# Splitting a carried projection over two positions, and loading the first band ahead of most weights, in a windowed-attention and convolution kernel

## The chip, the cores and the metric

The kernel runs on one core of one Trainium2 chip, as one launch. The metric is the device time in microseconds. The kernel before took 3295.52 us in the median of three runs (3294.91 to 3316.36).

## The reference

Input x is 4 x 128 x 128 x 128 (image, channel, row, column), float32. Layer 0 cuts each image into 9 x 9 overlapping regions of 16 x 16 pixels (step 14) and runs attention in each; overlaps are averaged. A projection, a depthwise convolution with batch statistics and a second projection follow. Layer 1 is two quantised 3 x 3 convolutions.

```python
y = _ln(tok, ln1_g, ln1_b)
qkv = y @ w_qkv                       # q, k, v; 4 heads of 32 channels
attn = softmax(einsum('bhqd,bhkd->bhqk', q, k) * hd ** -0.5)
o = einsum('bhqk,bhkd->bhqd', attn, v)
tok = o @ w_out + b_out + tok
xf = merge(tok)                       # overlaps averaged
y = _ln(xf, ln2_g, ln2_b) @ w_p0 + b_p0          # 128 -> 256 channels
ym = depthwise_conv5x5(y, dw_k)
ym = gelu(gelu(batchnorm(ym)))
x1 = ym @ w_p2 + b_p2 + xf
out = bn(conv3x3(q4(bn(conv3x3(q4(x1), q4(w1)))), q4(w2))) + x1
```

## The kernel before

Channels lie on the 128 partitions. An image is worked in nine bands of 16 rows (t = 0 to 35 over the four images), a band in nine regions from left to right, called positions 0 to 8 here. Within the loop over t and j the order of work is written by hand: PE, ACT, DVE and SP run their instructions in program order (MANUAL, L39), POOL is scheduled. Per position: scores (L684), exponential on ACT (L692), sums of pairs on POOL and DVE (L702), the values of the position before (L747, L755, L767 to L774), and, for every second position, v for two regions (L670).

Beside the attention of band t, the function beside(t) hangs other work on the positions, as four lists each: after the scores, after the sums, and two at the end. That other work is

- ln1_chunks(t+1), two chunks a1 and a2 of nine steps: squares, variance, deviation, spread, second, then q and k projections (L458). The layernorm's per-pixel scale goes to DRAM from ACT's queue (row, L374) and comes back spread over all partitions through SP (xn, L379); L388 multiplies it in.
- post_chunks(t-1), two chunks b1 and b2 of eleven steps: the output projection (L510, L511), the second layernorm, then four p0 steps, each one projection with wp0 (L526), a copy from PSUM on ACT into one of four y buffers (L531), and a store of it to y2_d. y_00 and y_10 are the first row half, y_01 and y_11 the second. A y buffer is used again four p0 steps later and must have been stored by then.
- the depthwise convolution of an image whose bands are done, conv_steps: a first step that loads two tiles (begin), then steps that load two ahead and multiply (L611), copy (L618), take statistics (L622) and store (cv_d). Images 0 and 1 are spread over nine bands each (t from 10 and from 19), image 2 over five bands (t from 28); the last image's first part starts at t=33, its second at t=35. A band in which such a list is begun is called fresh.

The four p0 steps of b2 do not fit into their own band: beside() returns them in the list left, and the next call takes them as f. For t above 9, f stands whole in position 0, and the p0 steps of b1 stand in position 8. For t up to 9 another list (full) places them.

All of these share three PSUM banks called pm (ps_m). SP issues almost all DMAs in program order, a step's stores after the step that follows it (run, flush).

Ahead of the loop, L120 to L160 load weights and vectors, fold scales, biases and the layernorm's centring into wqkv and wp0 on PE and DVE with tiles and PSUM of their own; then the first x blocks are loaded (L412) and ln1_chunks(0) runs, its two chunks step by step in turn.

Of the kernel before, what the change touches and what calls it, by code (L numbers as in the profile page):

```python
# [8 lines left out]
F32 = mybir.dt.float32  # L9
F8 = mybir.dt.float8e4  # L10
AF = mybir.ActivationFunctionType
ALU = mybir.AluOpType
# [34 lines left out]
def layers(  # L47
# [52 lines left out]
    def vector(v, name):  # L100
        n = v.shape[0] // P
        t = const.tile([P, n], F32, name=name)
        nc.sync.dma_start(out=t, in_=v.rearrange("(h p) -> p h", p=P))
        return t
# [15 lines left out]
    nc.sync.dma_start(out=wqkv, in_=w_qkv)  # L120
    g1, b1 = vector(ln1_g, "g1"), vector(ln1_b, "b1")
    wo = const.tile([P, P], F32, name="wo")
    nc.sync.dma_start(out=wo, in_=w_out)
    bo = vector(b_out, "bo")
    g2, b2 = vector(ln2_g, "g2"), vector(ln2_b, "b2")
    wp0 = const.tile([P, 2, P], F32, name="wp0")
    nc.sync.dma_start(out=wp0, in_=w_p0.rearrange("p (h m) -> p h m", h=2))
    bp0 = vector(b_p0, "bp0")

    with (
        tc.tile_pool(name=f"prep_{tag}", bufs=1) as prep,
        tc.tile_pool(name=f"ps_p_{tag}", bufs=1, space=PSUM) as ps_p,
    ):
        center = prep.tile([P, P], F32, name="center")
        nc.vector.tensor_scalar(center, ident, -1.0 / P, None, ALU.add)
        nc.vector.tensor_scalar(wqkv[:, :P], wqkv[:, :P], float(HD) ** -0.5, None, ALU.mult)
        pb = ps_p.tile([P, 8], F32, name="pb")  # L140
        qb = const.tile([P, 1], F32, name="qb")
        nc.tensor.matmul(pb[:, 0:1], wqkv[:, :P], b1, start=True, stop=True)
        nc.vector.tensor_copy(qb, pb[:, 0:1])
        bv = prep.tile([P, 1], F32, name="bv")
        nc.tensor.matmul(pb[:, 1:2], wqkv[:, 2 * P :], b1, start=True, stop=True)
        nc.vector.tensor_copy(bv, pb[:, 1:2])
        nc.tensor.matmul(pb[:, 2:3], wo, bv, start=True, stop=True)
        nc.vector.tensor_tensor(bo, pb[:, 2:3], bo, ALU.add)
        for h in range(2):
            nc.tensor.matmul(pb[:, 3 + h : 4 + h], wp0[:, h, :], b2, start=True, stop=True)  # L150
        nc.vector.tensor_tensor(bp0, pb[:, 3:5], bp0, ALU.add)
        nc.vector.tensor_scalar(wqkv, wqkv, g1, None, ALU.mult)
        nc.vector.tensor_scalar(wp0, wp0, g2, None, ALU.mult)

        for w in (wqkv, wp0.rearrange("p h m -> p (h m)")):
            n = w.shape[1]
            pw = ps_p.tile([P, 3 * P], F32, name="pw")
            nc.tensor.matmul(pw[:, :n], center, w, start=True, stop=True)
            nc.vector.tensor_copy(w, pw[:, :n])


    quad = const.tile([P, HEADS], F32, name="quad")
# [12 lines left out]
    with ExitStack() as actx:  # L175
# [22 lines left out]
        def scratch(n):  # L198

            return up.tile([P, 32 * CW], F32, name="u")[:, :n]  # L200
# [208 lines left out]
        def load_rows(pool, name, t, r, n):  # L409
            b, i = bands[t]  # L410
            xt = pool.tile([P, LB * P], F32, name=name)
            nc.sync.dma_start(  # L412
                out=xt[:, : n * P].rearrange("p (r c) -> p r c", c=P),
                in_=x[b, :, i * STEP + r : i * STEP + r + n, :],
            )
            return xt
# [364 lines left out]
        def beside(t):  # L781

            one = list(early) if t else ln1_chunks(1)
            early[:] = ln1_chunks(t + 2) if t + 2 < T else []
            two = post_chunks(t - 1) if t else []
            had = len(todo)
            if t >= 2:
                b, i = bands[t - 2]  # L790
                if i == NR - 1 and b < B - 1:
                    todo.extend(conv_steps(b))
                    share[0] = NR if b < B - 2 else 5
                elif b == B - 1 and i == 4:
                    todo.extend(conv_steps(B - 1))
                    share[0] = 2
                elif b == B - 1 and i == 6:
                    todo.extend(conv_steps(B))
                    share[0] = 1

            fresh = len(todo) > had
            n = len(todo) // share[0] if fresh else -(-len(todo) // max(share[0], 1))
            conv = [todo.pop(0) for _ in range(n)]
            share[0] -= 1
            a1, a2 = one if one else ([None] * 9,) * 2
            b1, b2 = two if two else ([None] * 11,) * 2
            if t == T:
                return [
                    *conv, *left, *b1[:2], *b2[:2], b1[2], b1[3], b2[2], b2[3], b1[4], b2[4], b1[5], b2[5],
                    b1[6], *b1[7:], b2[6], *b2[7:],  # L810
                ]


            c = [[] for _ in range(NR)]
            d = [[] for _ in range(NR)]
            twice = len(conv) > NR
            for j in sorted((1, 3, 5, 7, 8, 4, 6, 2, 0)[: len(conv)]):
                c[j] = [conv.pop(0)]
                d[j] = [conv.pop(0)] if twice and j and conv else []
            x1 = lambda: fetch(t, 0)  # L820
            x2 = lambda: fetch(t, 1)
            f, left[:] = list(left), b2[7:]
            s1 = early[0][0] if early else None
            plan = [
                ([a1[1]], [], f, [*c[0], a1[2]]),
                ([], [a1[3], *c[1]], [], [a2[0]]),
                ([a2[1]], [a1[4]], b1[:2], [*c[2], a2[2]]),
                ([], [a2[3], *c[3]], [], [b1[2]]),
                ([b1[3]], [a2[4]], [*a1[5:], *b2[:2]], [*c[4], b1[4]]),
                ([], [b1[5], *c[5]], [], [b2[2]]),  # L830
                ([b2[3]], [b1[6]], a2[5:], [*c[6], b2[4]]),
                ([], [b2[5], x1, *c[7]], [], []),
                ([], [b2[6], x2], b1[7:], [*c[8], s1]),
            ]
            if t == 0:
                plan[0] = ([], [], [], [*c[0], *a1[:3]])
            if t <= NR:

                left[:] = [*b1[9:], *b2[7:]]
                full = (f[:3], f[3:], b1[:2], a1[5:7], a1[7:], b2[:2], a2[5:7], a2[7:], b1[7:9])  # L840
                plan = [(one, two, w, four) for (one, two, three, four), w in zip(plan, full)]
            return [(one, two, three, four + d[j]) for j, (one, two, three, four) in enumerate(plan)]
# [15 lines left out]
        share[0] = NR + 1  # L858
        for blk in row_blocks(0):
            xb[0, blk[0]] = load_rows(xp, "xt", 0, *blk)  # L860
        bng, bnb = vector(bn_g, "bng"), vector(bn_b, "bnb")
        wp2 = const.tile([P, 2, P], F32, name="wp2")
        nc.sync.dma_start(out=wp2, in_=w_p2.rearrange("(h p) m -> p h m", p=P))
# [2 lines left out]
        ga2, be2 = vector(gamma2, "ga2"), vector(beta2, "be2")  # L866
        with nullcontext() if safe else tc.manual_schedule(engines=MANUAL):
            ln1_begin(0)
            for steps in zip(*ln1_chunks(0)):
                run(steps)  # L870
            last = None
            for t in range(T):
                flush(len(stores))
                scores, halves, values_in, values = attention(t)
                if t + 1 < T:
                    ln1_begin(t + 1)
                for j, side in enumerate(beside(t)):
                    scores(j)
                    if last:
                        last()  # L880
                    run(side[0])
                    halves(j)
                    if j == 0 and t:
                        post_begin(t - 1)
                    run(side[1])
                    if j % 2 == 0:
                        values_in(j)
                    run(side[2])
                    run(side[3])
                    last = lambda j=j, values=values: values(j)  # L890
            last()
            post_begin(T - 1)
            flush(len(stores))

            bctx.close()
            tail += [actx.enter_context(tc.tile_pool(name=f"late{n}_{tag}", bufs=n)) for n in (1, 4)]
            all_w = [tail[0].tile([P, 3, 16, 32], F32, name=f"w{k}") for k in range(NCK)]
            for k in range(NCK // 2):
                weights(all_w[k], k, 0, 2, nc.sync.dma_start)
            run(beside(T))  # L900
            flush(len(stores))
            run(todo)
            for n, s in enumerate(conv_steps(len(units) - 1, 4, (all_w, tail[1]))):
                s()
                flush(len(stores), nc.scalar)
                if n < NCK // 2:
                    weights(all_w[NCK // 2 + n], NCK // 2 + n, 0, 2, nc.sync.dma_start)
            flush(len(stores))
# [381 lines left out]
```

## Time and profile before

| | us |
|---|---|
| median of three runs | 3295.52 |
| profiled execution | 3291.11 |
| its span | 3289.0 |
| first scores (L684) start | 33.13 |
| last band's first scores start | 2104.7 |
| PE idle before L526, all | 37.2 |
| PE idle before L684, all | 20.3 |
| ACT idle before L531, all | 146.1 |
| POOL busy | 828.3 |

The rows of the page below are read as line, engine, operation, output and inputs, shapes and count, then busy time and mean duration, then the idle time of that engine just before these instructions and what ended most of it. Idle time of an engine counts only where it holds up the one that sets the end.

```profile
L526 PE MATMUL pm<-xn,wp 128*128 128x512 f32 (+1 forms) x576 | 249.7, 565 | 37.2 <-ACT y L531 20.0
L531 ACT ACTIVATE y<-pm,bp 128x512 f32<-128x512 f32 (+1 forms) x288 | 183.0, 641 | 146.1 <-DMA y_d<-y 80.3
```

### The profile page before, as it was taken

To read this page: it belongs to the slowest core of one execution; us is meant where nothing else is said; L and a number is where in the kernel's file an instruction comes from. 1 tells how busy PE (TensorE), PEld (TensorE's weight loads), DVE (VectorE), ACT (ScalarE), POOL (GpSimd) and SP (SyncE) were. 2 spreads that over 40 slices of the span, in tenths; PEclk is the share of its full clock that TensorE was granted. 3 is DMA by queue.
4 is the path that set the end of the run, shared out by engine and by line. 5 is a ranking of instruction groups with operands and counts; after the bars stand their busy time and mean duration, and the time that the engine had idled before them with its cause. 6 is when DMAs were issued, how large, how long until landed. Compare 5 with 4: busy or idle time off the path is not lost.

```text
span 3289.0 us, 75777 instructions
## 1 busy us (share of the span) xinstructions
PE 3093.5 (94%) x30922; PEld 1541.3 (47%) x30922; DVE 2020.6 (61%) x3247; ACT 1992.0 (61%) x2670; POOL 828.3 (25%) x1042
## 2 busy tenths in 40 slices
PE   7999999999999999999998998884799999999998
PEld 4555554444544444544444444553444444444343
DVE  5777887776766667676555664542455555666543
ACT  5777776777777676777565564532477767333443
POOL 3444443333333333333222222210111111000000
PEclk9999999999999999999999998876699999999999
DMA  3455677888886788886899888766799999452298
GB/s 93 135 172 159 174 181 179 194 211 196 210 198 166 182 205 208 198 211 166 190 202 206 206 192 202 191 169 176 242 356 360 359 357 300 150 167 71 99 359 311
DMA packets 812363, 682.76 MB, mean 208 GB/s; under 512 B 581646, under 2 KB 696679, under 8 KB 812007
## 3 DMA queue, kind: packets, MB, share of 16 engines
q1 hardware_dynamic: 793447, 673.10, 74.8%
q10 hardware_dynamic: 18560, 4.72, 0.6%
q8 instruction: 247, 4.05, 0.5%
q14 instruction: 109, 0.89, 0.1%
HBM read 410.81 MB, written 270.81 MB: 207 GB/s over the span
## 4 chain that ended last, share of the span: by engine, by line
PE 77%; DMA 10%; ACT 5%; DVE 3%; SPq 2%; issue 2%; ACTq 0%; POOL 0%; DVEq 0%; POOLq 0%
PE pc L1064 19%; PE pm L611 9%; PE sc L684 9%; PE po L747 8%; PE pm L458 6%; PE pb L1122 6%; PE pm L526 5%; PE pm L670 4%; PE po L755 4%; DMA y_d<-y 3%; PE pm L510 3%; PE pm L357 3%; DMA xn<-row 2%; DMA cv_d<-c 2%; DMA u<-y_d 2%
## 5 line engine op out<-in xcount | busy, mean ns | idle before, releaser
L767 DVE RECIPROCAL rd<-po 128x256 f32<-128x256 f32 x324 | 569.3, 1757 | 451.2 <-PE po L755 448.3
L1064 PE MATMUL pc<-q,wq 128*128 128x512 fp8e4 x3168 | 702.0, 381 | 14.4 <-DVE q L1076 14.4
L692 ACT ACTIVATE pt<-sc 128x1024 f32<-128x1024 f32 x648 | 628.1, 1025 | 129.3 <-PE sc L684 65.1
L702 POOL TENSOR_TENSOR sm<-pt 128x512 f32<-128x512 f32 x324 | 412.9, 1274 | 1048.1 <-ACT pt L692 706.8
L1064 PEld LDWEIGHTS <-wq 128*128 128x128 fp8e4 x3168 | 309.0, 98 | 417.7 <-issue 50.2
L684 PE MATMUL sc<-q,kr 32*128 32x256 f32 x5184 | 405.1, 415 | 20.3 <-ACT pt L692 20.1
L611 PE MATMUL pm<-u,w 40*32 40x504 f32 (+5 forms) x7680 | 369.1, 504 | 33.8 <-DMA u<-y_d 20.8
L684 PEld LDWEIGHTS sc<-q,kr 32*128 32x128 f32 x5184 | 250.1, 190 | 259.3 <-issue 166.1
L747 PE MATMUL po<-pt,v 128*32 128x256 f32 x5184 | 361.5, 398 | 8.7 <-DVE part L771 7.7
L618 ACT COPY c<-pm 128x512 f32<-128x512 f32 (+1 forms) x256 | 132.0, 563 | 264.4 <-PE pm L611 254.4
L622 DVE BATCH_NORM_STATS2 st<-c 128x6 f32<-128x512 f32 (+2 forms) x384 | 174.6, 505 | 190.1 <-ACT c L618 189.5
L526 PE MATMUL pm<-xn,wp 128*128 128x512 f32 (+1 forms) x576 | 249.7, 565 | 37.2 <-ACT y L531 20.0
L531 ACT ACTIVATE y<-pm,bp 128x512 f32<-128x512 f32 (+1 forms) x288 | 183.0, 641 | 146.1 <-DMA y_d<-y 80.3
L458 PE MATMUL pm<-xn,wqkv 128*128 128x512 f32 (+1 forms) x576 | 251.5, 565 | 11.6 <-DVE xn L388 9.0
L702 DVE TENSOR_TENSOR sm<-pt 128x512 f32<-128x512 f32 x324 | 243.5, 751 | 29.7 <-ACT pt L692 29.5
L611 PEld LDWEIGHTS pm<-u,w 40*32 40x32 f32 x7680 | 145.2, 112 | 216.8 <-issue 161.4
L1122 PE MATMUL pb<-cv,wp 128*128 128x512 f32 x512 | 232.6, 598 | 11.4 <-ACT cv L1113 11.4
L747 PEld LDWEIGHTS po<-pt,v 128*32 128x32 f32 x5184 | 139.6, 111 | 182.7 <-issue 108.7
L1072 DVE BATCH_NORM_STATS2 st<-pc 128x6 f32<-128x512 f32 x256 | 165.6, 689 | 67.3 <-PE pc L1064 67.3
L755 PE MATMUL po<-sm,ones 128*32 128x256 f32 x2592 | 206.0, 390 | 0.0
L670 PE MATMUL pm<-wqkv,yr 128*128 128x128 f32 x1296 | 193.4, 290 | 0.0
L670 PEld LDWEIGHTS pm<-wqkv,yr 128*128 128x128 f32 x1296 | 159.0, 192 | 68.7 <-issue 44.4
(147 smaller groups left out, 3410.8 us busy)
## 6 DMA issues: line engine op xcount, KB each, us to landing
cv<-cv_d SPq DMA_DIRECT2D x64, 1024.0 KB
u<-y_d SPq DMA_DIRECT2D x224, 256.0 KB
cv_d<-c SPq DMA_DIRECT2D x192, 256.0 KB
xn<-row SPq DMA_DIRECT2D x80, 512.0 KB
y_d<-y SPq DMA_DIRECT2D x160, 256.0 KB
xfl<-xf_d SPq DMA_DIRECT2D x64, 512.0 KB
id_d<-y SPq DMA_DIRECT2D x64, 512.0 KB
idt<-id_d SPq DMA_DIRECT2D x64, 512.0 KB
```

The lines of the kernel that those rows point to most:

```text
L458: nc.tensor.matmul(pm[:, : n * P], wqkv[:, m * P : (m + 1) * P], held["xn"][hh], start=True, stop=True,)
L526: nc.tensor.matmul(pm[:, : n * P], wp0[:, h, :], held["xn"][hh], start=True, stop=True)
L611: nc.tensor.matmul(pc[half][32 * q : 32 * q + 32, j, :, a:z], wt[hs, s, c0 + c, :], ut[hs, :, c, a + s - 1 : z + s - 1], start=(s == 1), s ...
L670: nc.tensor.matmul(pv[:, m, c, :], region(yr, j + m)[:, c * P : (c + 1) * P], wqkv[:, 2 * P :], start=True, stop=True,)
L684: nc.tensor.matmul(sc[h // 2][:, h % 2, kc, :].rearrange("p (r c) -> p r c", c=RS), region(kr, j)[hs, kc * P : (kc + 1) * P], queries(j, h ...
L692: nc.scalar.activation(pt, sc[p], AF.Exp)
L702: add(sm, pt[:, :, 0, :], pt[:, :, 1, :], ALU.add)
L747: nc.tensor.matmul(po[hs, 0, :], v[:, kc, hs], pt[h // 2][:, h % 2, kc, :], start=(kc == 0), stop=(kc == 1),)
L755: nc.tensor.matmul(po[hs, 1, :], ones, sm[h // 2][:, h % 2, :], start=True, stop=True)
L767: nc.vector.reciprocal(rd, po[:, 1, :])
L1064: nc.tensor.matmul(pc[:, h], w[:, t, :], q1[b][:, r + dy : r + dy + RB, dx : dx + P], start=(t == 0), stop=(t == 8),)
L1122: nc.tensor.matmul(pb[:, m], wp2[:, h, :], cv[:, h, px], start=(h == 0), stop=(h == 1))
```

## The change

Three things are moved; no operation on data is dropped. The loads of wo, bo, g2, b2, wp0 and bp0 come after the first two x loads on SP. The folding of the weights becomes two functions: prepare_qkv runs after the first layernorm step of band 0, prepare_rest after the fourth; their PSUM is taken from pm and the centring matrix from a u buffer. And in beside(), for t above 9, the carried list f is cut into two steps for position 0 and the rest for position 2, ahead of the output projection there, except in a fresh band of the last image. In fresh bands the convolution's steps take positions 3, 5, 7, 8, 4, 6, 1, 2, 0 in this order of preference, instead of 1, 3, 5, 7, 8, 4, 6, 2, 0.

```diff
-    nc.sync.dma_start(out=wo, in_=w_out)
-    bo = vector(b_out, "bo")
-    g2, b2 = vector(ln2_g, "g2"), vector(ln2_b, "b2")
...
-    bp0 = vector(b_p0, "bp0")
...
+    def prepare_qkv(pb, pw, center):
+        nc.vector.tensor_scalar(wqkv[:, :P], wqkv[:, :P], float(HD) ** -0.5, None, ALU.mult)
         nc.vector.tensor_scalar(center, ident, -1.0 / P, None, ALU.add)
...
+        nc.tensor.matmul(pb[:, 1:2], wqkv[:, 2 * P :], b1, start=True, stop=True)
         nc.vector.tensor_copy(qb, pb[:, 0:1])
...
+        nc.vector.tensor_scalar(wqkv, wqkv, g1, None, ALU.mult)
+
+        nc.tensor.matmul(pw[:, : 3 * P], center, wqkv, start=True, stop=True)
+        nc.vector.tensor_copy(wqkv, pw[:, : 3 * P])
+
+    def prepare_rest(pb, pw, center):
+        w = wp0.rearrange("p h m -> p (h m)")
         nc.tensor.matmul(pb[:, 2:3], wo, bv, start=True, stop=True)
...
+        nc.tensor.matmul(pw[:, : 2 * P], center, w, start=True, stop=True)
+        nc.vector.tensor_copy(w, pw[:, : 2 * P])
...
-            for j in sorted((1, 3, 5, 7, 8, 4, 6, 2, 0)[: len(conv)]):
+            where = (3, 5, 7, 8, 4, 6, 1, 2, 0) if fresh else (1, 3, 5, 7, 8, 4, 6, 2, 0)
+            for j in sorted(where[: len(conv)]):
...
+            f0, f1 = (f, []) if fresh and bands[t - 2][0] == B - 1 else (f[:2], f[2:])
...
-                ([a1[1]], [], f, [*c[0], a1[2]]),
+                ([a1[1]], [], f0, [*c[0], a1[2]]),
                 ([], [a1[3], *c[1]], [], [a2[0]]),
-                ([a2[1]], [a1[4]], b1[:2], [*c[2], a2[2]]),
+                ([a2[1]], [a1[4]], [*f1, *b1[:2]], [*c[2], a2[2]]),
...
             xb[0, blk[0]] = load_rows(xp, "xt", 0, *blk)
+        nc.sync.dma_start(out=wo, in_=w_out)
+        bo = vector(b_out, "bo")
+        g2, b2 = vector(ln2_g, "g2"), vector(ln2_b, "b2")
+        nc.sync.dma_start(out=wp0, in_=w_p0.rearrange("p (h m) -> p h m", h=2))
+        bp0 = vector(b_p0, "bp0")
...
             ln1_begin(0)
-            for steps in zip(*ln1_chunks(0)):
+            center = scratch(P)
+            room = lambda: ps_m.tile([P, 512], F32, name="pm")
+            for n, steps in enumerate(zip(*ln1_chunks(0))):
                 run(steps)
+                if n == 0:
+                    prepare_qkv(room(), room(), center)
+                elif n == 3:
+                    prepare_rest(room(), room(), center)
```

More of the change, by code (lines that the diff above doesn't have):

```diff
@@ L122, in layers @@
     wo = const.tile([P, P], F32, name="wo")
-    nc.sync.dma_start(out=wo, in_=w_out)
-    bo = vector(b_out, "bo")
-    g2, b2 = vector(ln2_g, "g2"), vector(ln2_b, "b2")
     wp0 = const.tile([P, 2, P], F32, name="wp0")
-    nc.sync.dma_start(out=wp0, in_=w_p0.rearrange("p (h m) -> p h m", h=2))
-    bp0 = vector(b_p0, "bp0")
[L133 to L137, printed above, removed]
+    qb = const.tile([P, 1], F32, name="qb")
@@ L138, in layers @@
+    bv = const.tile([P, 1], F32, name="bv")
+    def prepare_qkv(pb, pw, center):
+        nc.vector.tensor_scalar(wqkv[:, :P], wqkv[:, :P], float(HD) ** -0.5, None, ALU.mult)
         nc.vector.tensor_scalar(center, ident, -1.0 / P, None, ALU.add)
-        nc.vector.tensor_scalar(wqkv[:, :P], wqkv[:, :P], float(HD) ** -0.5, None, ALU.mult)
-        pb = ps_p.tile([P, 8], F32, name="pb")
-        qb = const.tile([P, 1], F32, name="qb")
         nc.tensor.matmul(pb[:, 0:1], wqkv[:, :P], b1, start=True, stop=True)
+        nc.tensor.matmul(pb[:, 1:2], wqkv[:, 2 * P :], b1, start=True, stop=True)
@@ L143, in layers @@
         nc.vector.tensor_copy(qb, pb[:, 0:1])
-        bv = prep.tile([P, 1], F32, name="bv")
-        nc.tensor.matmul(pb[:, 1:2], wqkv[:, 2 * P :], b1, start=True, stop=True)
         nc.vector.tensor_copy(bv, pb[:, 1:2])
+        nc.vector.tensor_scalar(wqkv, wqkv, g1, None, ALU.mult)
[3 more added lines that the diff above has]
+        w = wp0.rearrange("p h m -> p (h m)")
@@ L147, in layers @@
         nc.tensor.matmul(pb[:, 2:3], wo, bv, start=True, stop=True)
-        nc.vector.tensor_tensor(bo, pb[:, 2:3], bo, ALU.add)
         for h in range(2):
             nc.tensor.matmul(pb[:, 3 + h : 4 + h], wp0[:, h, :], b2, start=True, stop=True)
+        nc.vector.tensor_tensor(bo, pb[:, 2:3], bo, ALU.add)
         nc.vector.tensor_tensor(bp0, pb[:, 3:5], bp0, ALU.add)
-        nc.vector.tensor_scalar(wqkv, wqkv, g1, None, ALU.mult)
         nc.vector.tensor_scalar(wp0, wp0, g2, None, ALU.mult)
[L155 to L159, printed above, removed]
+        nc.tensor.matmul(pw[:, : 2 * P], center, w, start=True, stop=True)
```

## The prediction

> **What bounds the kernel now.** I read the page's busy times first, then the list of waits, then a table by stretch of time, then the timeline of the worst stretch, and last the chain of waits there and at the start.
>
> ```profile
> PE 3093.5 (94%) x30922; PEld 1541.3 (47%) x30922; DVE 2020.6 (61%) x3247; ACT 1992.0 (61%) x2670; POOL 828.3 (25%) x1042
> ```
>
> TensorE is busy for 94% of a span of 3289.0 us, so about 195 us are idle, and only idle or half-speed PE time can be won by moving work that stays the same. The waits (engine and line, what released it: us in total, times, longest) tell which idle time the diff can touch:
>
> ```profile
> ACT y L531 <- DMA y_d<-y: 80.3, 64, 6.6
> PE sc L684 <- ACT pt L692: 20.1, 28, 3.7
> PE pm L526 <- ACT y L531: 20.0, 12, 4.5
> ```
>
> L526 is the carried projection, L531 its copy out of PSUM. That copy waits for an older store of the same y buffer to land, then PE waits for the copy. By stretch (us, busy time per engine with counts, granted clock, DMA share, GB/s), one undisturbed band (t=22) and bands 29 to 32:
>
> ```profile
> 1216.00:1273.00 57.00, 56.95 (x693) 28.69 (x692) 40.37 (x63) 41.24 (x63) 21.06 (x27) 1.00 0.85 205
> ...
> 1627.00:1704.00 77.00, 71.35 (x844) 34.27 (x836) 44.75 (x69) 44.83 (x69) 21.03 (x27) 0.93 0.92 202
> 1704.00:1778.00 74.00, 69.73 (x852) 33.13 (x836) 43.75 (x68) 44.63 (x69) 21.03 (x27) 0.95 0.91 204
> 1778.00:1859.00 81.00, 72.28 (x848) 34.16 (x844) 45.60 (x71) 44.87 (x70) 21.03 (x27) 0.94 0.91 203
> 1859.00:1930.00 71.00, 66.20 (x787) 32.23 (x788) 43.35 (x67) 43.62 (x67) 21.03 (x27) 0.95 0.89 207
> ```
>
> Band 22 is PE from end to end: nothing can be won there. Bands 29 to 32 have idle PE and a clock below full. Band 31's timeline shows how (start, us, engine, line; in brackets the idle time before):
>
> ```profile
> 1788.98 0.58 ACT L531 ACTIVATE y<-pm,bp 128x384 f32<-128x384 f32 x1 [5.61 <-DMA y_d<-y]
> ...
> 1789.62 1.39 PE L526 MATMUL pm<-xn,wp 128*128 128x384 f32 x2 [4.53 <-ACT y L531]
> ...
> 1797.93 0.58 ACT L531 ACTIVATE y<-pm,bp 128x384 f32<-128x384 f32 x1 [6.56 <-DMA y_d<-y]
> ...
> 1801.07 2.99 PE L684 MATMUL sc<-q,kr 32*128 32x256 f32 x16 [3.74 <-ACT pt L692]
> ```
>
> The first of the four copies waits 5.61 us, the last 6.56 us, and the Exp of position 1, queued behind it on ACT, is late by as much. The scores that follow take 2.99 us where an undisturbed group takes 1.15: half clock. The chain of waits names the same stores:
>
> ```profile
> 1785.79 4.89 DMA y_d<-y
> ...
> 1791.27 6.58 DMA y_d<-y
> ```
>
> **What the Trainium skill says.** "TensorE: Matmul & The Clock Gate", section "What's actually happening", has the PE clock fall to half after an idle window of about 3.4 us and return after a busy one. The trace agrees: 1800 to 1807 was granted 0.51 after these pauses, and 1807 to 1815 again 1.00. "DMA: Bandwidth & Descriptors", "Why small descriptors are slow (HBM only)", says that 256-byte pieces pay an overhead; y rows are stored in runs of 64 floats, 256 bytes, and the page agrees in kind: 581646 of 812363 packets are under 512 B, and the engines are 0.91 busy at 203 GB/s where late slices reach 359. Its "Issuing engines are not separate DMA queues" says that SP's and ACT's DMAs share the 16 engines, so a shorter ACT wait doesn't make the stores land sooner. No run here isolates that.
>
> **The change part by part.**
>
> (1) Start. On SP, the two x loads pass six DMAs (wo, bo, g2, b2, wp0, bp0), each 0.43 us and a 0.04 gap: issued at 2.11 instead of 4.96, 2.85 us earlier. The chain there runs x load, square at 12.51, variance, row store, spread, L388 at 24.34, 14 projection matmuls (7.92), first scores at 33.13: all on the second x block, so all moves by 2.85. The six passed loads issue 0.94 us later and are needed only after the third layernorm step, about 13 us: covered. prepare_qkv keeps its work (PE 0.56 + 0.59 + 1.65, DVE 1.75) between 3 and 9 us, while x is in flight. prepare_rest's PE 0.59 + 1.01 + 1.11 and DVE 0.16 + 0.15 + 0.35 + 0.42 go into the stretch where PE sat idle 7.43 us before L458; with round trips some 4 us, covered; uncovered it would cost that 4. POOL's queue is not passed. Three pm banks instead of private ones are rotated, all read long before reuse. **-3 us** (+1 to -4).
>
> (2) Bands 10 to 28. Cutting the timeline at the first score of each position, position 0 lasts 7.3 us when undisturbed (t=11, 15, 20, 22) and up to 8.9 otherwise; over these bands the excess sums to about 7 us, with ACT waits of 1 to 3 us for y stores in front of it. With two projections left there, PE no longer meets the late bank in position 0: I take 5 of 7. When an image's convolution starts beside regions (t=10, 19, 28), its steps go from positions 1, 3, 5 to 3, 5, 7 (t=28: 1,3,4,5,7,8 to 3,4,5,6,7,8). In t=19 position 7 has no step now, lasts 3.1 us, and position 8 has PE waiting 2.40 us for DVE's part (DVE waits 3.82 us for xn), then half clock: 11.6 us where others take 6.6 to 7.5. A step in position 7 gives xn time: -4. Against it, the first loads stand behind the y stores of position 2 on SP, and in t=28 the first product follows one position later: store issue to landing some 4 us, load 5, against about 10 us until position 4's end. I book +1. **-8 us** (+4 to -12).
>
> (3) Bands 29 to 32. A clean band with 7 convolution steps is 57.3 + 3 x 2.78 (one step on PE) = 65.6, with 6 steps 62.9. Measured by the cut: 77.2, 73.8, 80.6, 71.7: an excess of 43.6, of which 42 in positions 0 to 2 (115.9 us in the four bands against 4 x 18.5). In the changed band 31 the copy y_00 still waits until 1788.98, but PE goes on to scores and values until about 1787.3; the convolution step then wants the bank that y_00 frees at 1789.6: 2.3 us. ACT, without the other two copies, starts the Exp of position 1 at about 1792 instead of 1799.99; scores wait 0.8 more; I add 0.9 for some half clock. So 4 us stay of about 10.5 a band: -26. The two remaining copies come at about 1798, when the last store (1791.27 + 6.58 = 1797.85) has just landed. On SP their own stores now stand behind the a1 xn load and the next x load, and nothing needs them before position 8. But DMA: the four bands move 61.8 MB (stretch times rate), and the backlogged 1778 to 1807, in four stretches of 7, 6, 9 and 7 us at 231, 242, 204 and 201, moved 218 GB/s; at that rate 61.8 MB take 283 us of today's 303. I take that limit: **-20 us** (-6 to -38).
>
> (4) Band 34 also splits (33 and 35 do not, by the condition). It has waits of 1.46 for y, a 5.81 us ACT wait and 4.70 us for xf in position 2 whose root is the row store that ACT issues late, after the copy; 20 us ran at half clock. **-6 us** (+3 to -12). Bands 0 to 9 and everything after the bands: 0, as their order is unchanged.
>
> Moving two of four copies costs no PE, ACT or DVE time in itself: 1.38 us of ACT and about 1.8 us of PE go from position 0 to 2.
>
> Sum -37. The profiled execution was 3291.1 (span 3289.0 and 2.1 around it), which gives 3254; the median of the runs shown, 3295.5, stands 4.4 above it, and I forecast against the median: **3258.5 us**.
>
> **Rivals.**
> A, the forecast: 3246 to 3272. Chance 0.55.
> B, the DMA queue is the real bound: for: share 0.91, and 4 us slices above 1. Against: SP itself waits some 32 us a band on producers, so it isn't full all the time. Then y stalls return as late u loads at L611, and I halve or more the terms: -3 - 4 - 8 - 2 = -17, 3278. Chance 0.22.
> C, full release: half clock goes with the pauses and all positions take clean lengths: -3 - 11 - 36 - 10 = -60, 3235. Against: y_00 still waits. Chance 0.16.
> D, slower: position 2 overloads. It now turns over six pm tiles (variance, values, two p0, two wo) through three banks instead of four, and two are freed only by DVE's L511 (0.70 each), behind L388 (1.29). If PE waits w there in the 24 split bands, the gain is gone at w = 37/24 = 1.5 us; past 1.5 it decides, and at 3 us the kernel is at 3330. Against: in t=28 L511 ends at 1582.14, just as the next step starts at 1582.06, and two p0 ahead of it give DVE 1.8 us more. Chance 0.03.
> E, the split does nothing, because the wait only moves with the copies: only the start gains, 3292. Chance 0.04.
>
> **Numbers.** 1% is 33 us, about what a measurement of this kernel can tell from no change: the border is 3262.6. C and two thirds of A lie below it: 0.53. D alone is over the other: 0.03. The rest 0.44. The range 3236 to 3290 takes in A, B and half of C.
>
> **What would show it.** First scores near 30.3 us. Fewer than 25 us of ACT waiting for y stores in bands 29 to 32 (41.6 now). PE L526 waiting for L531 under 4 us in all. Positions 0 to 2 of these bands at about 90 to 98 us together instead of 115.9, granted clock 0.97 or more. Band 19's position 8 under 8 us. I am wrong if L611 waits for u instead (B), if L510 or L611 wait on xf or pm in position 2 (D), or if the first step of t=28 waits for its loads.

## The result, and the profile after

The changed kernel took 3324.34 us (median of 4 runs, 3321.94 to 3327.47), the kernel before 3297.88 (4 runs, 3294.91 to 3316.36): a ratio of 1.0061, 95% interval 1.004 to 1.0082. By the ratio it is 0.6% or some 20 us slower (the two medians lie 26.5 us apart), where 37 us less were forecast. A second set of runs gave 1.0057 (1.0041 to 1.0073). The profiled execution took 3324.55 us, its span is 3322.8.

The page of the changed kernel, busy times:

```profile
PE 3121.6 (94%) x30922; PEld 1544.0 (46%) x30922; DVE 2020.4 (61%) x3247; ACT 1992.4 (60%) x2670; POOL 827.8 (25%) x1042
```

As many matmuls as before, but PE is busy for 28.1 us longer (3093.5 before): the same work, much of it at a lower clock (granted 0.952 over the run, 0.958 before). DVE and ACT are unchanged. Its list of waits (engine and line, what released it: total us, times, longest):

```profile
DVE xn L381 <- DMA xn<-row: 103.2, 39, 15.5
...
ACT y L524 <- DMA y_d<-y: 60.4, 47, 5.9
...
PE pm L604 <- DMA u<-y_d: 29.6, 16, 7.2
```

(L524 was L531, L381 was L388, L604 was L611, L504 was L511, L519 was L526.) The y waits fell from 80.3 to 60.4 us as intended; those for xn (82.7 before) and for u (20.8 before) rose. By stretch (us, busy time per engine with counts, granted clock, DMA share, GB/s), band 22 and then bands 29 to 32:

```profile
1218.00:1275.00 57.00, 56.92 (x693) 28.71 (x692) 40.20 (x63) 41.06 (x63) 21.06 (x27) 1.00 0.91 202
1635.80:1720.80 85.00, 77.83 (x848) 34.83 (x840) 46.38 (x71) 44.97 (x69) 21.01 (x27) 0.90 0.95 200
1720.80:1796.00 75.20, 71.55 (x842) 32.90 (x839) 44.20 (x68) 44.66 (x69) 20.64 (x27) 0.93 0.86 194
1796.00:1876.80 80.80, 76.16 (x844) 34.18 (x836) 45.66 (x71) 44.75 (x69) 20.61 (x27) 0.89 0.89 194
1876.80:1953.40 76.60, 72.95 (x799) 32.63 (x791) 43.84 (x67) 43.90 (x67) 20.63 (x27) 0.89 0.87 194
```

Band 22 is as full as before. The four late bands take 317.6 us instead of 303.3, and their clock is 0.89 to 0.93 instead of 0.93 to 0.95. The waits of PE in just these bands, first of the kernel before:

```profile
PE pm L526 <- ACT y L531: 13.5, 4, 4.5
PE sc L684 <- ACT pt L692: 9.3, 5, 3.7
PE pm L611 <- DMA u<-y_d: 0.4, 1, 0.4
```

and of the changed kernel:

```profile
PE pm L604 <- DVE xf L504: 10.1, 4, 3.6
PE pm L604 <- ACT y L524: 5.0, 3, 2.1
PE pm L604 <- DMA u<-y_d: 2.8, 1, 2.8
PE sc L677 <- ACT pt L685: 0.8, 2, 0.6
```

The waits have moved from the projection and the scores to L604, the convolution. They sum to 18.7 us instead of 23.2: **PE waits less, and the bands are longer**. By my estimate the clock accounts for most of that: the missing clock, doubled, times the length of each stretch gives about 61 us at half clock, 34 before, and each such microsecond loses half of its work. So the four bands lost 4.5 us less to pauses, and some 13.7 us more to the half clock behind them: 9.2 of the 14.3 us; the other 5 us have no such plain place. A second profile of the changed kernel (e5 below) agrees in kind: the bands took 318.7 us, PE was idle for 23.9 us of them, about as long as before (23.4), and some 51 us were at half clock. That PE waits less is one profile's finding; that its waits did not grow and the half clock did is what both show.

Where the largest of the new pauses comes from, in the timeline of band 30 (start, us, engine, line; in brackets the idle time before):

```profile
1738.14 6.75 SPq L573 DMA_DIRECT2D u<-y_d  x4
...
1739.81 0.48 ACTq L367 DMA_DIRECT2D row<-rstd  x1
...
1740.07 1.15 PE L677 MATMUL sc<-q,kr 32*128 32x256 f32 x16
...
1746.78 1.46 SPq L405 DMA_DIRECT2D xt<-in_x_dram  x1
1748.33 0.98 SPq L391 DMA_DIRECT2D y_d<-y  x2
1749.40 0.71 SPq L391 DMA_DIRECT2D xf_d<-xf  x1
...
1750.17 0.73 SPq L372 DMA_DIRECT2D xn<-row  x1
...
1757.58 1.03 DVE L381 TENSOR_TENSOR xn<-xn,xt 128x384 f32<-128x384 f32 x2 [6.08 <-DMA xn<-row]
...
1758.52 1.14 DVE L504 SCALAR_TENSOR_TENSOR xf<-pm,bo,xr 128x384 f32<-128x384 f32 x2
...
1759.19 3.61 PE L604 MATMUL pm<-u,w 40*32 40x512 f32 x32 [3.57 <-DVE xf L504]
```

Read from the end: PE waits 3.57 us for a PSUM bank that DVE's xf (L504) frees; xf stands behind the xn multiply (L381); that waits for the second block's xn load; and the load, whose row store was issued at 1739.81, is issued on SP's queue at 1750.17, 10.1 us after the scores of position 3 began (5.0 us in band 30 of the kernel before, 1731.27 to 1736.23). Right in front of it stand the two y stores that the split moved to position 2, and the xf store. The chain of waits goes the same way:

```profile
1750.17 7.39 DMA xn<-row
...
1758.61 0.54 DVE xf L504
```

In bands 30, 31 and 32 this pause lies in position 4 (3.57, 2.48 and 1.74 us); the fourth wait on xf, 2.31 us in band 29, lies in position 3 and goes back in the same way to the load of the first block.

The two y stores took only 0.98 us of SP's time themselves. SP's queue was held up more farther ahead, at 1738.14: 6.75 us for four loads of u, where the four at 1727.29 in the kernel before took 1.62. SP's waits in bands 29 to 32, of the kernel before:

```profile
SPq L580 <- DMA row<-rstd: 22.0, 6, 6.1
```

and of the changed kernel:

```profile
SPq L573 <- DMA row<-rstd: 43.9, 10, 6.2
```

L573 loads u, which has nothing to do with a row. The trace names the semaphore that tells of each DMA's landing: in this program the DMAs of SP and ACT share eight of them in turn, and the u load that SP issues at 1744.19 has, and waits for, the one of the row store of 1739.81. In bands 29 to 32 of the kernel before, nothing on SP's queue met the second block's row store before its own xn load did; in the changed kernel SP meets it 6, 8, 6 and 8 DMAs ahead of that load.

Outside these bands: first scores at 31.1 us (33.1), band 19 shorter by 4.9 us, but band 20 longer by 7.5, band 28 by 4.6, band 34 by 5.3.

### The profile page after: what moved, and what is told of

The parts are those of the page before. It is cut to its first block, busy times and chain, and to the rows that moved or that the text cites. A ratio compares the mean times of both kernels' runs of the same rounds, so it can differ in the third digit from the quotient of the medians.

```text
span 3322.8 us, 75779 instructions
## 1 busy us (share of the span) xinstructions
PE 3121.6 (94%) x30922; PEld 1544.0 (46%) x30922; DVE 2020.4 (61%) x3247; ACT 1992.4 (60%) x2670; POOL 827.8 (25%) x1042
## 4 chain that ended last, share of the span: by engine, by line
PE 77%; DMA 10%; ACT 5%; DVE 3%; SPq 3%; issue 2%; ACTq 1%; POOL 0%; DVEq 0%
PE pc L1071 19%; PE pm L604 10%; PE sc L677 9%; PE po L740 8%; PE pb L1129 6%; PE pm L451 6%; PE pm L519 6%; PE pm L663 4%; PE po L748 4%; PE pm L350 3%; PE pm L503 2%; DMA y_d<-y 2%; DMA u<-y_d 2%; ACT pt L685 2%; DMA cv_d<-c 2%
## 5 line engine op out<-in xcount | busy, mean ns | idle before, releaser
L1071 PE MATMUL pc<-q,wq 128*128 128x512 fp8e4 x3168 | 701.5, 381 | 14.4 <-DVE q L1083 14.4
L604 PE MATMUL pm<-u,w 40*32 40x504 f32 (+5 forms) x7680 | 395.2, 518 | 63.9 <-DMA u<-y_d 29.6
L611 ACT COPY c<-pm 128x512 f32<-128x512 f32 (+1 forms) x256 | 132.9, 564 | 310.9 <-PE pm L604 282.4
L519 PE MATMUL pm<-xn,wp 128*128 128x512 f32 (+1 forms) x576 | 253.9, 563 | 20.5 <-DVE xn L381 17.5
L604 PEld LDWEIGHTS pm<-u,w 40*32 40x32 f32 x7680 | 146.7, 114 | 265.3 <-issue 180.0
L524 ACT ACTIVATE y<-pm,bp 128x512 f32<-128x512 f32 (+1 forms) x288 | 183.3, 642 | 135.6 <-PE pm L519 69.2
```

The lines of the kernel that those rows point to most:

```text
L519: nc.tensor.matmul(pm[:, : n * P], wp0[:, h, :], held["xn"][hh], start=True, stop=True)
L604: nc.tensor.matmul(pc[half][32 * q : 32 * q + 32, j, :, a:z], wt[hs, s, c0 + c, :], ut[hs, :, c, a + s - 1 : z + s - 1], start=(s == 1), s ...
L1071: nc.tensor.matmul(pc[:, h], w[:, t, :], q1[b][:, r + dy : r + dy + RB, dx : dx + P], start=(t == 0), stop=(t == 8),)
```

## The experiments

Three theories. **T1**: the stores moved into position 2 make the second block's xn load late. **T2**: the new list of convolution positions does the harm: it pushes bytes into the bands that follow. **T3**: the DMA engines are the bound, and whatever is freed comes back as another late transfer. Ratios are against the kernel before on the same chip (6 to 22 runs of each form); that kernel's medians there were 3299 to 3305 us, where the expectations below still reckon with 3298, and its single runs lay from 3287 to 3315. Band lengths are of one profile each, cut at the first scores of the bands, and a profiled execution lies up to 15 us from its kernel's median: two profiles of the changed kernel gave 317.6 and 318.7 us for bands 29 to 32, and three kernels with one order there gave 303.3 (before), 306.4 (e1) and 307.6 (e4). The runs are called e1 to e15 in their order.

**The parts, one by one.** Start alone (e1), against the changed kernel:

```diff
-            where = (3, 5, 7, 8, 4, 6, 1, 2, 0) if fresh else (1, 3, 5, 7, 8, 4, 6, 2, 0)
-            for j in sorted(where[: len(conv)]):
+            for j in sorted((1, 3, 5, 7, 8, 4, 6, 2, 0)[: len(conv)]):
...
-            f0, f1 = (f, []) if fresh and bands[t - 2][0] == B - 1 else (f[:2], f[2:])
+            f0, f1 = f, []
```

> Only the reordered start; the carried projection whole in position 0 and the old list of convolution positions. Every theory: the first scores at 31.1 us as in the changed kernel (33.1 before), everything behind them as before, so about 2 us under the kernel before (3296 for 3298), and 26 us under the changed kernel.

Measured: 3309.73 for 3304.7, ratio 1.0011 (1.0 to 1.0022); first scores at 30.7 us. The 2 us at the start are there in every profile; in the total they can't be seen. What made the total no shorter stays open.

Start and new list (e2), with `f0, f1 = f, []`:

> The start and the new list of convolution positions for fresh bands; the carried projection whole in position 0. Theory T1 (the split's moved stores make the second block's xn load late in bands 29 to 32): the list costs little, 3294 to 3304 us, and the y waits of bands 29 to 32 stay near 41 us. Theory T2 (the list pushes loads and stores of bands 19 and 28 into the next bands, which then run short of DMA): 3315 us or more, with t=28 to 32 some 15 us longer than before. Theory T3 (the DMA engines bound bands 29 to 32 whatever the order): within 4 us of the start alone.

Measured: 1.0035 (1.0023 to 1.0046), some 8 us over the start alone. Band 19 took 56.0 us (63.0 in the start alone), band 20 61.9 (57.2), band 28 71.4 (64.8). In band 19 9.3 MB were moved and in band 20 12.4, where the start alone has 11.0 and 10.9: T2's mechanism is real. The time itself, 3315.62 us, is within T2's range, but the kernel before took 3304.7 there; the 11 us over it lie between T1's figures and T2's. The y waits of bands 29 to 32 were 30.1 us.

Start and split, old list (e3), `f0, f1 = (f, []) if fresh else (f[:2], f[2:])`:

> The start and the split in all bands that are not fresh; the old list of positions. T1: nearly the whole loss is here, 3312 to 3325 us; SyncE's waits for a row store near 60 us in bands 29 to 32 as in the changed kernel (34 before), and matmuls of position 4 that wait for DVE xf. T2: 3285 to 3295 us, since the y waits go (42 to about 20 us in bands 29 to 32) and nothing else moves. T3: 3293 to 3300, the y waits traded one for one for late loads.

Measured: 1.0021 (1.0011 to 1.0032), 3310.7 us, just under T1's range and far over T2's; over the kernel before it is some 7 us, half of the least that T1 asks. Its new waits are T1's, 7.5 us of L604 on xf and 4.9 on y, SP's waits of u loads for a row store are 45.3 us, and bands 29 to 32 took 313.5 us. But "nearly the whole loss" is not here: list and split each carry a part.

The split in the early bands only (e4), `f0, f1 = (f, []) if fresh or t > 28 else (f[:2], f[2:])`, old list:

> As the start and the split, but in bands after the 28th the projection stays whole in position 0. T1: the loss is gone, 3290 to 3297 us, bands 29 to 32 as in the kernel before. T2: 3290 to 3296 too (no new list); T3 the same. If the loss stays above 3305 us, it comes from the ordinary bands, and all three are wrong.

Measured: 1.0002 (0.9992 to 1.0012), 3306.83 us; bands 29 to 32 at 307.6 us. That is over the 3305 us that would speak against all three theories, but the kernel before took 3304.7 there: by the ratio the loss is gone. In the ordinary bands the split costs nothing and may gain some 3 us over the start alone (the intervals overlap); the split's loss, some 6 us between e3 and e4, belongs to the late ones.

The changed kernel once more (e5), on the chip of the next runs:

> The changed kernel itself, on the chip on which its parts are compared, to set its loss beside theirs: about 0.6% slower than before. If its parts add up, it stands 0.24% (the new list over the start alone) and 0.1% (the split) above the start alone; a larger distance is an interaction of the two.

Measured: 1.0057 (1.0041 to 1.0073). Start, list and split give 0.11 + 0.24 + 0.10 = 0.45% when added; the rest, if there is any, is interaction.

**T1 by itself.** The changed kernel, with only the two stores held back in the late bands (e6):

```diff
+            if t > 28:
+                f1 = [lambda s=s: aside(s) for s in f1]
...
-                ([], [a2[3], *c[3]], [], [b1[2]]),
+                ([], [a2[3], issue, *c[3]], [], [b1[2]]),
```

`aside` runs a step and sets its store apart, `issue` sends those to SP's queue behind the xn load of a2[3].

> The changed kernel, with the two y stores of position 2 kept back, in bands after the 28th, until the second block's xn load has been issued in position 3. T1 (those stores in front of the xn load make it late): the stalls of pm on DVE xf in position 4 (2.3, 3.6, 2.5 and 1.7 us in bands 29 to 32) fall under 1 us each, with the half clock behind them, and the time falls by 8 to 15 us against the changed kernel. T3 (the DMA engines are full in these bands, so that SyncE's queue is late whatever stands in it): within 4 us of the changed kernel, with the stalls still there or in another place.

Measured: 1.0017 (1.0007 to 1.0028), 0.40% or 13 us under the changed kernel. Bands 29 to 32 took 301.7 us. PE's waits there:

```profile
PE pm L604 <- DMA u<-y_d: 5.9, 5, 2.5
PE pm L604 <- ACT y L524: 3.3, 2, 1.7
PE pm L604 <- DVE xf L504: 2.5, 2, 2.3
```

The waits on xf fell from 10.1 to 2.5 us. Those in position 4 are gone, as expected; one of 2.3 us is left, in position 3 of band 31, behind the first block. Time at half clock fell from 61 (51 in the second profile) to 37.5 us. In band 30 the xn load is issued 7.1 us after position 3 began (10.1 in the changed kernel). In bands 31 and 32 position 3 itself is longer; counted from the start of position 4, the load comes 2.1, 1.9, 0.5 and 2.8 us later in the four bands, where the changed kernel has 3.1, 4.9, 3.2 and 2.9, and in the kernel before it comes ahead of position 4 in all four. So it is earlier, but far from as early as before. SP still meets the row store 4, 6, 4 and 6 DMAs ahead of the load, just the two fewer; the part of the shared semaphores alone was not tried. All of DVE's waits for xn together did not fall (40.8 us, 40.4 in the changed kernel): those ahead of the next band's layernorm fell from 23.8 to 16.3, those of the second layernorm grew. T1 holds for the second block's load. Waits for u grew from 2.8 to 5.9: T3's sort, and smaller.

The same aim by another way (e7): the load on another queue, from band 29 on (`t > 29`) and for the second block only:

```diff
-                nc.sync.dma_start(
+                (nc.gpsimd if late else nc.sync).dma_start(
                     out=xn[:, :n].rearrange("p (q w) -> p q w", q=4),
```

> The changed kernel, with the second block's xn load of bands 29 and later issued by GpSimd instead of SyncE, so that nothing of SyncE's stands in front of it. T1: no stall of pm on DVE xf in position 4 of bands 29 to 32, their half clock at 35 us or less (61.5 in the changed kernel), time 10 to 15 us under the changed kernel. T3: the xn load lands late all the same, since it shares the engines; within 4 us. A third way: GpSimd, in order, stands at the load until the row has landed, and its sums and copies are late: new waits on POOL and a slower kernel.

Measured: 1.0024 (1.0014 to 1.0034), 11 us under the changed kernel; bands 29 to 32 at 301.2 us, 27.3 of them at half clock, no wait on xf in position 4 and one of 2.3 us in position 3. GpSimd issues the load ahead of position 4 in all four bands, as SP does in the kernel before, and PE waited for none of GpSimd's sums there. Two ways to get the load out early, one result.

**What the y waits were worth.** The projection whole in position 0 as before, start reordered, y stores from band 28 on issued on ACT's queue (e8):

```diff
-                    store(
...
+                    if 27 <= t < T - 1:
+                        nc.scalar.dma_start(out=out, in_=src)
+                    else:
+                        store(out, src)
```

(`out` and `src` are the two arguments of that store.)

> The reordered start alone (projection whole in position 0), with the y stores of the bands from the 28th on issued by ScalarE right behind their eviction, so that SyncE's queue no longer stands before them. If the y waits are a matter of order in SyncE's queue, they fall from 41 to under 10 us in bands 29 to 32, and the time falls by about 20 us, as my sum for the split had it. T3: the stores land as late as before, or the time that they free comes back as late u, xn or xr loads; within 5 us of the start alone.

Measured: 1.0008 (0.9997 to 1.002), equal to the start alone. The y waits of bands 29 to 32 are gone, 1.5 us for 41.6, and the bands still took 303.8 us: positions 0 to 2 fell to 80.6 us (117.5 in the start alone), and positions 3 to 8 rose to 223.3 (189.0), much as in the changed kernel. What PE and DVE wait for there:

```profile
PE pm L606 <- DVE xf L504: 10.0, 5, 4.1
```

```profile
DVE xn L381 <- DMA xn<-row: 41.6, 13, 5.6
```

(L606 is the convolution.) The wait for xn in these bands of the kernel before:

```profile
DVE xn L388 <- DMA xn<-row: 17.9, 8, 4.9
```

With the y stall gone, the xn load is late next, and the same kind of pause on xf appears without any split, mostly in position 3 (8.8 of the 10.0 us), behind the first block's load. So the time that y frees comes back elsewhere, as T3 has it, and freeing y alone shows no gain, whoever does it.

Both at once (e9): y stores on ACT's queue as in e8 and, from band 29 on, all four xn loads of a band on GpSimd's:

> The y stores of the bands from the 28th on issued by ScalarE (as in the run before of that kind), and all four xn loads of these bands by GpSimd, so that neither a y store nor an xn load has anything of SyncE's in front. Without the y waits bands 29 to 32 still took 304 us. If what took their place is order in SyncE's queue (xn loads that wait behind others: VectorE waits 42 us for xn there), these bands fall to about 285 us and the kernel to 0.4 to 0.6% below the kernel before. T3 (the DMA engines, 92% busy in band 29 of the kernel before, are the bound): 298 us or more in these bands, within 0.2% of the kernel before. GpSimd held up by its waits would show as waits on POOL and a slower kernel.

Measured: bands 29 to 32 at 290.7 us, 10.2 at half clock, xn waits down to 13.7 us:

```profile
DVE xn L381 <- DMA xn<-row: 13.7, 12, 1.8
```

In these profiles the order of the queue, with all bytes as before, was worth 13 to 16 us in these bands; 290.7 us lies between the 285 expected and T3's 298. GpSimd did hold PE up a little: 4.0 us of waits for its sums. Yet the total is 1.0002 (0.9984 to 1.002), as T3 had it. Band 34 took 100.7 us, 89.6 before; but it took 98.4 in the start alone, so where the gain went is not settled.

T3 directly: 3.7 MB of stores left out of these bands, once with the y stores on ACT's queue (e10) and once without (e11). Bands 2 to 5 store as many bytes more:

```diff
-                    if hh:
-                        store(
...
+                    if hh and not 28 <= t <= 31:
+                        store(xf_d[b][:, px], held["xf"][:, : n * P])
+                    if hh and 1 <= t <= 4:
+                        store(xf_d[b + 3][:, px], held["xf"][:, : n * P])
```

> The y stores issued by ScalarE, and the xf stores of bands 29 to 32 left out there (their eight blocks are stored in early bands, from other rows, so that the output isn't the reference's): 3.7 MB of some 62 MB less in these bands, about 16 us of the engines' time. T3: bands 29 to 32 fall from 304 us to 288 to 294, the kernel by 10 us or more. If capacity is not what binds, they fall by less than 4 us.

> The reordered start alone, with the same xf stores left out: the control. Its y waits stay in part. T3: it gains too, but less than the kernel without y waits, 4 to 10 us. If it gains as much, the traffic binds through the y stores themselves, and the wait on y was only where the full engines showed.

Measured: the totals, 1.0044 and 1.0049, are no help, since bands 0 to 9, which took the extra stores, grew by 10 and 15 us over the same kernels without. Bands 29 to 32 took 298.4 us (303.8 with all stores) and 302.0 (306.4): 5.4 and 4.4 us, hardly more than the 4 us by which profiles of one order differ. The first is less than the 10 to 16 that a pure engine bound asks for; the second lies in T3's range for the control. Capacity may matter; order mattered more.

The change's own parts at their best, the stores held back and the old list (e12):

> The start, the split, the two stores kept back until the xn load, and the old list of convolution positions. From the parts: held stores took 0.4% off the changed kernel, the old list should take 0.2% more: 0.1% below to 0.05% above the kernel before. This is the best that the change's own parts give, if the readings so far are right.

Measured: 0.9988 (0.9976 to 1.0), as expected. Bands 29 to 32 took 302.5 us and kept 5.8 us of waits on xf, most of them in position 3. So: holding the stores takes 0.40%, the old list another 0.29%, and what is left of the change (start, split) is then some 4 us faster than before, with an interval that reaches no change.

**A kernel faster than both.** The kernel before, no part of the change, only the queues of bands 29 to 32: the y stores of the output bands 28 to 31 on ACT's, xn loads on GpSimd's (e13).

> The kernel before, with nothing of the change, but in bands 29 to 32 alone the y stores issued by ScalarE and the xn loads by GpSimd. If my forecast's worth of the stalls in these bands (20 us) was right and only its means wrong, the bands fall from 303 to about 290 us here too, bands 33 to 35 stay as before (281.7 us), and the kernel is 10 to 14 us below the kernel before (0.9956 to 0.997). If the engines' capacity takes it back, the work that these bands no longer delay crowds bands 33 to 35, which grow by as much: within 0.1% of before.

Measured: 0.9974 (0.9962 to 0.9987), 3293.05 for 3301.15, just short of the forecast. Bands 29 to 32 took 293.4 us, bands 33 to 35 some 2 us more than before. With start and early split added (e14):

> The reordered start and the split in the ordinary bands (up to the 28th, not in fresh ones), and in bands 29 to 32 the same change of queues with the projection whole. If the gains add, 3 us (split) and 2 us (start) below the run before: 0.994 to 0.997. If what the queues gain is given back in bands 33 to 35: 0.999 to 1.001.

Measured: 0.9981 (0.997 to 0.9993): neither range was met, and the gains don't add. Bands 29 to 32 took 298.2 us. And e13 with the y stores of one output band more on ACT's queue (`27 <= t <= 31`, e15):

> As the run on the kernel before with changed queues, with one band's y stores more (those evicted in positions 6 and 8 of band 28 and position 0 of band 29). There band 29 kept its y wait: 2.5 us on y, 3.2 us on the Exp behind it, and 10.2 us of half clock, 10.8 us by my way of counting. If such a stall is worth its idle time and half of the half-clock time, band 29 falls from 80.5 to about 71 us, as in the run that had this store changed too (71.0), and the kernel to 0.994 to 0.9965. If the engines' capacity takes it back in bands 30 to 35: 0.997 to 0.998.

Measured: **3284.28 for 3300.43, ratio 0.9956 (0.994 to 0.9973)**. Band 29 fell from 80.5 to 75.5 us, less than the 71 expected, the kernel as far as expected. Its stretches for bands 29 to 32:

```profile
1628.30:1703.90 75.60, 72.99 (x844) 34.41 (x840) 46.22 (x69) 45.44 (x70) 23.13 (x31) 0.95 0.93 215
1703.90:1777.80 73.90, 71.48 (x842) 33.77 (x839) 45.05 (x69) 44.73 (x69) 22.91 (x31) 0.95 0.90 207
1777.80:1850.30 72.50, 69.78 (x843) 33.35 (x839) 44.76 (x69) 44.91 (x69) 22.36 (x31) 1.00 0.93 215
1850.30:1917.30 67.00, 65.28 (x796) 31.23 (x792) 43.39 (x67) 43.86 (x67) 22.40 (x31) 1.00 0.94 219
```

288.9 us for 303.3; 13.7 us at half clock for 34.1. The same bytes went in less time: 207 to 219 GB/s for 202 to 207, at a DMA share of 0.90 to 0.94 for 0.89 to 0.92. The gain of 14.4 us in these bands is as large as the kernel's, 0.44% of 3300; that all of it comes from there isn't shown, since the two profiled executions lie only 4.3 us apart, and in them bands 33 to 35 took 6 us more than before.

## Why the prediction was wrong, by its own steps

The sum was -37 us and came out at about +20 (33.4 between the two profiled executions, of which that of before lies below all four of its runs). By the experiments, that is 11 to 13 us for the stores and the late xn load of the bands from 29 on (e6, e7) and 8 to 10 us for the list.

**(1) Start, -3.** Right in kind: the first scores come 2.0 us earlier, 31.1 where 30.3 were named. In the total of the start alone nothing is seen of it (1.0011).

**(2) Bands 10 to 28, -8.** Failed on the list. Band 19's position 8 went from 11.6 to 6.6 us, as named, and band 19 gained 4.9; but that was luck in part. The stall that the -4 was read from stands in the profile of before alone: in the eleven other profiles with the old list, position 8 took 7.5 to 8.1 us. And the convolution's steps that are put later load and store later too, and band 20 moves 12.6 MB instead of 10.7: its positions 1 and 2 took 20.0 us where an undisturbed split band has 12.8, and it lost 7.5. In band 28 position 4 took 16.7 us (13.0), with waits for u of 0.44 and 0.92 us and 6.8 us of half clock. I had booked +1 for all that. The losses of these two bands show in every profile: with the new list (five) band 20 took 60.1 to 64.7 us and band 28 70.5 to 73.0, with the old (twelve) 57.2 to 57.5 and 64.8 to 70.3. The list by itself costs 8 us (e2 against e1), and 10 where the stores are held (e6 against e12). The 5 us booked for position 0 don't show either: the 15 bands that neither begin a list nor follow t=19 took 864.9 us together before, and 863.0 to 874.4 in the eight profiles with the split. (Position 0 of t=10 took 9.7 us, not 8.9 at most.)

**(3) Bands 29 to 32, -20: the step that failed.** Its first half was right: positions 0 to 2 of the four bands went from 116 to 94 us, where 90 to 98 were named; PE's wait for y at L519 is no longer in the list of these bands; y waits are 19.9 us, under the 25 named. It booked positions 3 to 8 at nothing, and they went from 187 to 224 us. The sentence that failed is "On SP their own stores now stand behind the a1 xn load and the next x load, and nothing needs them before position 8". Nothing needs those stores, but the second block's xn load stands behind them; that was not looked at. Holding them back gave 13 us (e6). And the cost that was taken off with the y wait, the pause and the half clock behind it, was no worth of the wait alone: e8 frees it wholly and gains nothing, because the xn load, 17.9 us of wait before, is late next at 41.6. I read this as the y stall giving SP's queue the time to catch up; that reading was not tried by itself. The limit of 218 GB/s was not the one reached: the changed bands ran at 194 to 200.

**(4) Band 34, -6.** Came out at +5.3, with 5.16 us of L604 on xf in position 2 (4.70 before) and 3.87 on y in position 0. But it took 89.6, 98.4 and 90.1 us in the kernels before, e1 and e4, which have the same order there, so its share is not settled.

**The rivals.** B (the DMA queue binds, u loads late at L604) had the right family, since the next transfer was late, but not the transfer (xn, then xf, 10.1 us; u only 2.8), nor the sign: 3278. D (bank waits through xf) named L504 as the releaser and the mechanism by which it freezes PE, but placed it in position 2 and priced it by DVE's work; it came in position 4 (once in 3), through a late load, and had been given 0.03. It would have ranked higher with one question asked: what is queued on SP behind the two stores? C (full release) had positions 0 to 2 nearly right and nothing else, and E (only the start gains) didn't come. Of the signs named, y waits, L519, positions 0 to 2 and band 19 came true, and the first scores nearly; the granted clock (0.97 named, 0.89 to 0.93 measured) said that it had failed. Of the three signs of being wrong, two showed: the first product of t=28 waited for its loads (0.44 and 0.92 us), and the convolution's waits for u rose from 20.8 to 29.6 us in all, 0.4 to 2.8 in bands 29 to 32, too little for B.

## What to carry to other kernels

When a step moves, follow every DMA that it issues down its queue to the next load that something waits for; a store that nobody needs can still make a load late. A stall that is long in a loop of full queues can be cover for the next transfer: before booking its whole length, ask which load was on time only because of it, and free both together (e8 and e9: 303.8 and 290.7 us for the same bands). And price a pause with the half clock behind it: here pauses that were no longer in sum, but lay in the convolution, were followed by 51 to 61 us of half clock instead of 34. That their place is the reason was not tried by itself.

## What the hardware showed that was not expected

- Pauses much shorter than a window were followed by half clock. The Trainium skill, "TensorE: Matmul & The Clock Gate", section "What's actually happening", has the clock fall after an idle window of about 3.4 us. In the changed kernel, from the first scores to 2000 us, half clock began within 5 us after the start of 7 of 8 pauses of PE above 1.75 us (the eighth, of 1.80 us, stands at 34 us), of 4 of 13 between 0.75 and 1.75, and of 1 of 25 between 0.3 and 0.75. Only one of these pauses is longer than 3.4 us. The half-clock times fit the page's window: 3.4, 6.8, 10.2 and 13.7 us. Pauses at L604, whose matmuls use 40*32 of the array, were mostly followed by 6.8 to 10.2 us, those at the projection and the scores in bands 29 to 32 of the kernel before by 3.4 to 6.8; that the small tiles are the cause was not tried.
- The same skill's "DMA: Bandwidth & Descriptors", section "Issuing engines are not separate DMA queues", says that starting DMAs from several engines saves only the sequencer's time to start them, usually small. Here it took the y waits of four bands from 41.6 to 1.5 us (e8), and with the xn loads 0.44% off the kernel (e15). What was saved is not only the start of a DMA but its place behind others that wait: SP waited some 33 us of each of these bands in the kernel before.
